# First image of a two-layer attention network: order of normalising and table eviction, and where and when the bias rows are loaded and turned

## The chip, the cores and the metric

The kernel runs on one core of one Trainium2 chip. The metric is the device time of one execution in microseconds, as the median of several runs. The engines are TensorE (PE, matrix products; PEld is its weight loading), VectorE (DVE), ScalarE (ACT), GpSimd (POOL) and SyncE (SP), which here only issues DMAs. Each engine works through its own list of instructions in order, and semaphores hold an instruction until what it needs is there.

## The reference, cut to what matters

There are two layers on x of shape (8, 384, 32, 32). The change lies in the first one: group norm, attention of 8 heads of 48 over 1024 tokens with a relative bias, an output product and a residual.

```python
rel = (coords[:, None, :] - coords[None, :, :]) / denom      # coords of 32 x 32 positions
bias = gelu(rel @ mlp_w1 + mlp_b1) @ mlp_w2 + mlp_b2         # (1024, 1024, 8)
qkv = tokens(_gn(x)) @ qkv_w + qkv_b
attn = softmax(einsum('bhnd,bhmd->bhnm', q * scale, k) + transpose(bias, (2, 0, 1)))
x = x + from_tokens(einsum('bhnm,bhmd->bhnd', attn, v) @ proj_w + proj_b)
```

The bias of a pair of positions depends only on their distance in both directions, so that 63 x 63 = 3969 values for each of the 8 heads hold all of it. The second layer (a second attention and a feed-forward part) is untouched.

## The kernel before, in words

**Table and bias rows.** The 3969 bias values per head come out of a small perceptron at the start: `hidden(r)` computes the hidden units of half r of the distances on TensorE, with a gelu on ScalarE; `table_part(r, hids)` (L272 to L291) multiplies them with the second matrix, evicts the sum on VectorE in reversed order (`part`, L284) and stores it with four DMAs to the table in DRAM (L288). From the table, `grow` is built in SBUF: for each of 128 partitions (4 rows of 32 keys) and each head, 60 rows of 32 bias values. A quarter of a head, 15 rows, is a *part*; there are 8 x 4 = 32 parts. `grow_part(h, c)` (L293 to L308) takes a tile `wide` of the pool of score tiles, fills it with four DMAs of 114.2 KB, each shifted by one element per partition (L300), and then copies it reversed, or *turned*, into its place in `grow`: on ScalarE for even quarters (L306), on VectorE for odd ones (L308). One pool of nine buffers (`etile`) holds hidden units, `wide` tiles and exponentials of scores.

**Group norm.** `group_norm(b, xn)` returns five stages: the statistics of the three channel blocks on VectorE (L323, three stages; the third also sends them through DRAM so that groups stand together, L327 and L331), `scatter`, which combines them on VectorE and POOL and sends scale and shift back (L345, L349), and `apply`, which normalises three blocks (L353), for image 0 on VectorE, for the others on POOL.

**Projection and units.** `project_qk` computes three pairs of heads for queries and keys (L372, six blocks of twelve products; queries are evicted on VectorE, L382, keys on ScalarE, L386) and after each pair rearranges rows by two DMAs (L389); the fourth pair is gathered out of these rows. `project_v` computes the values in four blocks (L400, L405). An image's attention then is 32 *units* (4 pairs x 2 halves of the queries x 4 groups of keys). `scores` makes two PSUM tiles of scores (L426), adds the bias (L437, VectorE) and takes exponentials (L441, ScalarE); `weigh` (L457), two units later, multiplies with the values. The four PSUM tiles of two banks each are shared by all products. After the eighth unit of a pair, its outputs go to `oT[:, pair]` (L465, L468) and `divide` sends the row sums to DRAM and back (L483, L485), inverts them on POOL (L486), stores them (L487) and later spreads and multiplies them (L494, L498).

**What sets the order.** The order on every engine is written out by hand (`manual_schedule`): instructions stand in the order in which the Python code issues them. `later.after(n, work)` issues `work` at the n-th next `later.step()`. In image 0 there are six steps in `project_qk`, four in `project_v` and one after each unit, so that step 11 follows unit 0. The dependences between instructions are found from what they read and write. All DMAs here are issued on SP's queue, in this order too.

Before the change the parts are issued whole (load, then turn) at steps 1 to 22: two at each of the first ten steps, one at each of the other twelve. Image b + 1 is loaded after unit 1 of image b, and its group norm stages come 5, 6, 7, 10 and 13 steps on.

Of the kernel before, what the change touches and what calls it, by code (L numbers as in the profile page):

```python
# [27 lines left out]
P = 128  # L28
QP = P // 2
B, C, IH, IW = 8, 384, 32, 32  # L30
# [10 lines left out]
NF0 = NP0 - 1  # L41
# [3 lines left out]
RW = 2 * IW - 1  # L45
# [51 lines left out]
def _layer0(tc, ins, x1, flag):  # L97
# [6 lines left out]
    with ExitStack() as ctx:  # L104
# [8 lines left out]
        def mm2(name):  # L113
            return ps.tile([P, NH, HALF], F32, tag="p", name=name)

        def etile(name, shape=(P, N)):
            return ep.tile(list(shape), F32, tag="e", name=name)
# [4 lines left out]
        later = _Later()  # L122
# [10 lines left out]
        def backwards(last, *dims):  # L133

            dims = [(1, n) if isinstance(n, int) else n for n in dims]
            return bass.AP(last.tensor, last.offset, [last.ap[0]] + [[-s, n] for s, n in dims])
# [13 lines left out]
        for g in range(P // QT):  # L150
            at = g * QN
            n = min(QN, NREL - at)
# [48 lines left out]
        def place_weights_qk():  # L201
            whole = 2 * NF0 * D0
            for s in range(2):
                nc.vector.tensor_copy(
                    wqk[:, :, s, :, 0:D0],
                    raw[:, :, s, 0:whole].rearrange("p k (h d) -> p k h d", d=D0),
                )
                for j in range(2):
                    at = whole + j * D0
                    nc.vector.tensor_copy(  # L210
                        wqk[:, :, s, j::2, D0:S0],
                        raw[:, :, s, at : at + D0].rearrange("p k (c d) -> p k c d", d=FR),
                    )

        def load_bias_qk():
            with nc.allow_non_contiguous_dma(reason="a bias, once"):
                for j in range(2):
                    for row, n, at, step in (
                        (j * S0, D0, j * D0, 2 * D0),
                        (j * S0 + D0, FR, (2 * NF0 + j) * D0, FR),  # L220
                    ):
                        for s in range(2):
                            nc.sync.dma_start(
                                bqk[row : row + n, s],
                                bass.AP(
                                    qkv_b.tensor, qkv_b.offset + s * C + at, [[1, n], [step, NF0]]
                                ),
                            )

        def load_weights_v_out():  # L230
            nc.sync.dma_start(wv, qkv_w[:, 2 * C : 3 * C].rearrange("(k p) c -> p k c", p=P))
            nc.sync.dma_start(bv, qkv_b[2 * C : 3 * C].partition_broadcast(P))
            pw = ins["L0_conv_proj_w"]
            for j in range(2):
                last = (2 * NF0 + j) * D0
                for row, n, at, step in (
                    (j * S0 + SP, D0, j * D0, 2 * D0),
                    (j * S0, FR, last, FR),
                ):
                    nc.sync.dma_start(  # L240
                        wp[row : row + n],
                        bass.AP(
                            pw.tensor, pw.offset + at * C, [[C, n], [step * C, NF0], [1, C]]
                        ),
                    )
                nc.sync.dma_start(wl[j * S0 + SP : (j + 1) * S0], pw[last : last + D0])
            with nc.allow_non_contiguous_dma(reason="a bias, once"):
                nc.sync.dma_start(bp, ins["L0_conv_proj_b"].rearrange("(k p) -> p k", p=P))

        oT = const.tile([P, NP0, N], F32, tag="oT", name="oT")  # L250
        sums = const.tile([P, B, NP0, 2 * N // P], F32, tag="sums", name="sums")

        WR = GW // 4

        def hidden(r):

            hids = {}
            for k in range(2):
                for a in range(2):
                    ph = mm2(f"ph{r}{k}{a}")  # L260
                    for i in range(2):
                        g = 2 * a + i
                        nc.tensor.matmul(
                            ph[0:HC, i], w1[g * QT : g * QT + 2, ts(k, HC)],
                            rel[g * QT : g * QT + 2, ts(r, HALF)], start=True, stop=True,
                        )
                    hid = etile(f"hid{r}{k}{a}", (HC, 2, HALF))
                    nc.scalar.activation(
                        hid.rearrange("p i q -> p (i q)"), ph[0:HC].rearrange("p i q -> p (i q)"),
                        AF.Gelu, bias=b1[:, k : k + 1],  # L270
                    )
                    hids[k, a] = hid  # L272
            return hids

        def table_part(r, hids):
            pb = mm2(f"pb{r}")
            for k in range(2):
                for g in range(P // QT):
                    nc.tensor.matmul(
                        pb[ts(g, QT), 0], w2[:, k, :], hids[k, g // 2][:, g % 2],  # L280
                        start=(k == 0), stop=(k == 1),
                    )
            part = etile(f"part{r}", (P, HALF))
            nc.vector.tensor_scalar_add(backwards(part[:, HALF - 1 : HALF], HALF), pb[:, 0], b2)  # L284
            for g in range(P // QT):
                at = g * QN + r * HALF
                n = min(HALF, NREL - at)
                nc.sync.dma_start(  # L288
                    table[:, NREL - at - n : NREL - at],
                    part[g * QT : g * QT + H0, HALF - n : HALF],  # L290
                )  # L291

        def grow_part(h, c):  # L293

            run = (WR - 1) * RW + IW
            wide = etile(f"wide{h}_{c}", (P, WR, RW))
            for dy in range(QROWS):
                src = table[h : h + 1, :]
                at = src.offset + NREL - 1 - (WR * (c + 1) + QROWS - 2 - dy) * RW - 2 * (IW - 1)
                nc.sync.dma_start(  # L300
                    wide[ts(dy, IW)].rearrange("p w c -> p (w c)")[:, :run],
                    bass.AP(src.tensor, at, [[1, IW], [1, run]]),
                )
            turned = backwards(wide[:, WR - 1, IW - 1 : IW], (RW, WR), IW)
            if c % 2 == 0:
                nc.scalar.copy(grow[:, h, ts(c, WR), :], turned)  # L306
            else:
                nc.vector.tensor_copy(grow[:, h, ts(c, WR), :], turned)  # L308
# [237 lines left out]
        with tc.manual_schedule():  # L546
            stages = group_norm(0, first)
            for stage in stages[:3]:
                stage()
            place_weights_qk()  # L550
            hids = [hidden(r) for r in range(2)]
            stages[3]()
            load_bias_qk()
            for r in range(2):
                table_part(r, hids[r])
            stages[4](nc.vector)
            load_weights_v_out()
            parts = [(h, c) for h in range(H0) for c in range(4)]

            def grow_parts(n):  # L560
                for _ in range(n):
                    grow_part(*parts.pop(0))

            for i in range(22):
                later.after(i + 1, lambda i=i: grow_parts(2 if i < 10 else 1))
            qk = project_qk(0, first)
            project_v(0, first)
            for b in range(B):
                held = []
                for i, u in enumerate(units):  # L570
                    done = held.pop(0) if len(held) == LAG else None
                    held.append(
                        (u, scores(b, qk, u, lambda: weigh(b, *done) if done else None))
                    )
                    if i == 1 and b + 1 < B:
                        xn = load(b + 1)
                        for at, stage in zip((5, 6, 7, 10, 13), group_norm(b + 1, xn)):
                            later.after(at, stage)
                    if i == 3 and b > 0:
                        project_out(b - 1)  # L580
                    later.step()
                if b + 1 < B:
                    qk = project_qk(b + 1, xn)
                for done in held:
                    finish = weigh(b, *done)
                    if finish is not None:
                        finish()
                if b + 1 < B:
                    project_v(b + 1, xn)
            project_out(B - 1, apart=True)  # L590
# [1062 lines left out]
```

## Time and profile before

| what | before |
|---|---|
| median of 3 runs | 3165.62 us (3164.66 to 3168.25) |
| the profiled execution's own time | 3169.41 us |
| its span from the first to the last instruction | 3166.5 us |
| TensorE busy | 3057.7 us (97%) |
| VectorE, ScalarE, POOL busy | 1744.7, 1400.7, 458.8 us |
| mean granted TensorE clock | 0.988 |
| q1, the queue of SP's DMAs | 147.41 MB |

A row of the profile that describes a group reads: start in us, busy time in us, engine, line, operation, output <- input, count, and in brackets how long the engine was idle before it and what ended this. In the table of stretches, each row is a window, its length, the busy time of each engine with its number of instructions, the granted TensorE clock as a share of full speed, the mean busy share of the 16 DMA engines and GB/s. The stages of image 0 in this execution: projection from 28.12, values from 60.79, scores from 76.37, and the projection of image 1 at 217.68 us.

### The profile page before, as it was taken

The page shows a single profiled execution, that of the slowest core. Times are in us where ns is not written, and L with a number is a line of the kernel's source. Part 1 is how long each engine was busy: PE and PEld are TensorE (multiplying, and loading weights), DVE is VectorE, ACT ScalarE, POOL GpSimd, SP SyncE. Part 2 cuts the span into 40 slices and gives each one's busy share as a digit, 9 for nine tenths or more (in the row PEclk, how much of TensorE's full clock was granted, in tenths as well). Part 3 has the DMA queues.
Part 4 walks back from the last instruction along what each step waited for, and adds up shares of the span by engine and source line. Part 5 has one row for each costly group of instructions (what it writes and reads, how often), then busy time and mean ns, then how long its engine had stood idle before and what let it go on. Part 6 is the DMA issues. An engine that isn't in the chain of part 4 may idle for free.

```text
span 3166.5 us, 46012 instructions
## 1 busy us (share of the span) xinstructions
PE 3057.7 (97%) x19066; PEld 1572.0 (50%) x19066; DVE 1744.7 (55%) x1748; ACT 1400.7 (44%) x1763; POOL 458.8 (14%) x302
## 2 busy tenths in 40 slices
PE   8799999999999999996899999999999999999999
PEld 3254645455555546432445645645645555634343
DVE  2554737373645647273464764754754854844545
ACT  2452616252543526162272462553553643643535
POOL 0110202111111102021200301301201201211110
PEclk9899999999999999998999999999999999999999
DMA  7302020211212020203310110100101101101011
GB/s 178 107 18 79 22 82 16 69 35 25 73 23 81 19 79 22 62 16 105 75 42 22 44 33 22 62 17 21 61 22 27 51 22 29 53 18 62 15 49 42
DMA packets 102768, 150.49 MB, mean 48 GB/s; under 512 B 62260, under 2 KB 65828, under 8 KB 101784
## 3 DMA queue, kind: packets, MB, share of 16 engines
q1 hardware_dynamic: 99688, 147.41, 16.5%
q8 instruction: 153, 2.51, 0.3%
q14 instruction: 63, 0.52, 0.1%
q10 hardware_dynamic: 2864, 0.05, 0.1%
HBM read 111.05 MB, written 27.32 MB: 44 GB/s over the span
## 4 chain that ended last, share of the span: by engine, by line
PE 42%; DVE 4%; DMA 3%; ACT 2%; issue 1%; POOL 1%; SPq 0%; DVEq 0%; ACTq 0%; POOLq 0%
PE s L1168 11%; PE o L1217 10%; PE y2p L1419 5%; PE pq L1023 5%; PE pp L1279 4%; PE y1p L1365 3%; PE pv L1104 3%; POOL hc L1073 1%; PE sum L1240 1%; DVE lun L1319 1%; DVE un L1314 1%; DVE un L1311 1%; DMA rb<-rd 1%; PE tsa L992 1%; PE hs L1052 0%
## 5 line engine op out<-in xcount | busy, mean ns | idle before, releaser
L441 ACT ACTIVATE e<-e 128x1024 f32<-128x1024 f32 x512 | 534.8, 1056 | 461.6 <-DVE e L437 445.6
L437 DVE TENSOR_TENSOR e<-s,grow 128x1024 f32<-128x1024 f32 x512 | 601.1, 1218 | 190.6 <-PE s L426 186.9
L426 PE MATMUL s<-qk 48*64 48x512 f32 x4096 | 613.8, 595 | 23.3 <-DVE e L437 20.3
L457 PE MATMUL o<-e,v 64*64 64x512 f32 x4096 | 608.5, 592 | 0.0
L1179 ACT ACTIVATE e<-s,kc 128x512 f32<-128x512 f32 x768 | 463.5, 691 | 213.3 <-PE s L1168 195.3
L1168 PE MATMUL s<-qk,qk 64*64 64x512 f32 x3072 | 400.6, 601 | 9.9 <-DVE v L1114 9.1
L1217 PE MATMUL o<-e,v 64*64 64x512 f32 x3072 | 391.6, 591 | 0.2 <-ACT e L1179 0.2
L426 PEld LDWEIGHTS s<-qk 48*64 48x64 f32 x4096 | 232.3, 133 | 259.4 <-issue 92.8
L457 PEld LDWEIGHTS o<-e,v 64*64 64x64 f32 x4096 | 249.3, 134 | 192.6 <-issue 96.2
L1194 DVE TENSOR_TENSOR t<-t,e 128x1024 f32<-128x1024 f32 x192 | 231.3, 1222 | 79.2 <-ACT e L1179 79.2
L1023 PE MATMUL pq<-bx,L_attn_qkv_wT 128*128 128x512 f32 x576 | 254.4, 596 | 2.3 <-DVE L_attn_qkv_wT L979 2.1
L372 PE MATMUL pq<-xn,wqk 128*128 128x512 f32 x576 | 251.0, 597 | 1.8 <-DVE xn L353 1.8
L1168 PEld LDWEIGHTS s<-qk,qk 64*64 64x64 f32 x3072 | 146.0, 134 | 211.5 <-issue 128.2
L486 POOL TENSOR_TENSOR inv<-sums,over 128x16 f32<-128x16 f32 x32 | 92.9, 2904 | 1033.1 <-DMA sums<-sd 927.1
L1217 PEld LDWEIGHTS o<-e,v 64*64 64x64 f32 x3072 | 138.8, 133 | 191.4 <-issue 164.6
L372 PEld LDWEIGHTS pq<-xn,wqk 128*128 128x128 f32 x576 | 109.4, 191 | 143.6 <-issue 142.9
L1023 PEld LDWEIGHTS pq<-bx,L_attn_qkv_wT 128*128 128x128 f32 x576 | 107.7, 190 | 145.7 <-issue 140.4
L1191 DVE TENSOR_TENSOR t<-e,e 128x1024 f32<-128x1024 f32 x96 | 114.1, 1224 | 84.1 <-ACT e L1179 84.1
L1352 DVE TENSOR_REDUCE parts<-y 128x1 f32<-128x1024 f32 x75 | 90.0, 1218 | 95.2 <-ACT y L1349 95.0
L1073 POOL TENSOR_TENSOR hc<-hc,rsqrt 128x32 f32<-128x32 f32 x24 | 135.3, 5639 | 2.0
L1039 ACT ACTIVATE qsq<-pq 128x1024 f32<-128x1024 f32 x48 | 49.1, 1024 | 192.5 <-DVE qk L1033 92.1
L1104 PE MATMUL pv<-L_attn_qkv_wT,bx 128*128 128x384 f32 x384 | 130.9, 497 | 1.9 <-DVE meanL_ffn_W1T L1144 1.9
(149 smaller groups left out, 2935.3 us busy)
## 6 DMA issues: line engine op xcount, KB each, us to landing
rb<-rd SPq DMA_DIRECT2D x112, 256.0 KB
wide<-table SPq DMA_DIRECT2D x128, 114.2 KB
xn<-in_x_dram SPq DMA_DIRECT2D x24, 512.0 KB
res<-in_x_dram SPq DMA_DIRECT2D x24, 512.0 KB
x<-res SPq DMA_DIRECT2D x24, 512.0 KB
bx<-x SPq DMA_DIRECT2D x8, 1536.0 KB
rq<-hi SPq DMA_DIRECT2D x48, 256.0 KB
out_dram<-bx SPq DMA_DIRECT2D x24, 512.0 KB
```

Of the source, the lines that this page charges most:

```text
L372: nc.tensor.matmul(pq[:, h], wqk[:, k, s, 2 * pair : 2 * pair + 2, :].rearrange("p h d -> p (h d)"), xn[:, k, ts(h, HALF)], start=(k == 0) ...
L426: nc.tensor.matmul(s[j][ts(c, QP), i], qk[pair][rows, 1, ts(4 * m2 + 2 * i + c, QP)], qk[pair][rows, 0, ts(h, HALF)], start=True, stop=True,)
L437: nc.vector.tensor_add(e.rearrange("p (i q) -> p i q", i=2), s[j], bass.AP(near.tensor, near.offset, [near.ap[0], [-QROWS * IW, 2], [1, HA ...
L441: nc.scalar.activation(e, e, AF.Exp)
L457: nc.tensor.matmul(po[ts(j, S0), r], v[keys, 2 * m2 + i, 2 * pair + j, :], es[j][keys, ts(i, HALF)], start=(m2 == 0 and i == 0), stop=(m2 ...
L1023: nc.tensor.matmul(pq[:, h], wqkv[:, k, s * C + pair * P : s * C + (pair + 1) * P], xt[:, k, ts(h, HALF)], start=(k == 0), stop=(k == KC - 1),
L1073: nc.gpsimd.tensor_tensor(c, c, rsqrt.to_broadcast(list(c.shape)), ALU.pow)
L1104: nc.tensor.matmul(pv[:, i, 0:C], xt[:, k].rearrange("c (p m) -> c m p", m=MT)[:, 2 * m2 + i], wqkv[:, k, 2 * C : 3 * C], start=(k == 0), ...
L1168: nc.tensor.matmul(s[j][ts(c, QP), i], qk[pair, 1][rows, ts(4 * m2 + 2 * i + c, QP)], qk[pair, 0][rows, ts(h, HALF)], start=True, stop=True,)
L1179: nc.scalar.activation(e[:, ts(i, HALF)], s[j][:, i], AF.Exp, scale=kc[:, pair, j, m : m + 1])
L1194: nc.vector.tensor_add(total[j], total[j], e)
L1217: nc.tensor.matmul(po[ts(j, D1), r], v[keys, 2 * m2 + i, at : at + D1], es[j][keys, ts(i, HALF)], start=(m2 == 0 and i == 0), stop=(m2 == ...
```

## The change

`table_part(1)` is issued at step 1, behind the first block of the projection, and image 0 is normalised before `table_part(0)`; the weights for the values and the output are loaded ahead of the stores of the table. `grow_part` is split into `grow_load`, which issues the four DMAs, and `grow_turn`, the reversed copy. Of the 32 parts, 21 are loaded into pool tiles as before, at steps 2 to 10 (3, 3, 2, 3, 2, 2, 2, 2, 2), and each group is turned one step after it was loaded. The other 11 are loaded at steps 9 to 19, one at a step, into `oT[:, 1]`, `oT[:, 2]` and `oT[:, 3]` in turn (the outputs of pairs 1 to 3 are written there later), and a turn follows two steps after its load, at steps 11 to 21. Parts are loaded and turned in one order, first in, first out. For image 0 only, the next image is loaded after unit 8 and not after unit 1, and its group norm moves with it.

```diff
-        def grow_part(h, c):
+        def grow_load(h, c, staged):
 
             run = (WR - 1) * RW + IW
-            wide = etile(f"wide{h}_{c}", (P, WR, RW))
+            wide = oT[:, staged, 0 : WR * RW] if staged else etile(f"wide{h}_{c}", (P, WR * RW))
             for dy in range(QROWS):
                 src = table[h : h + 1, :]
                 at = src.offset + NREL - 1 - (WR * (c + 1) + QROWS - 2 - dy) * RW - 2 * (IW - 1)
                 nc.sync.dma_start(
-                    wide[ts(dy, IW)].rearrange("p w c -> p (w c)")[:, :run],
-                    bass.AP(src.tensor, at, [[1, IW], [1, run]]),
-                )
-            turned = backwards(wide[:, WR - 1, IW - 1 : IW], (RW, WR), IW)
+                    wide[ts(dy, IW), 0:run], bass.AP(src.tensor, at, [[1, IW], [1, run]])
+                )
+            return wide
+
+        def grow_turn(h, c, wide):
+
+            last = (WR - 1) * RW + IW - 1
+            turned = backwards(wide[:, last : last + 1], (RW, WR), IW)
             if c % 2 == 0:
                 nc.scalar.copy(grow[:, h, ts(c, WR), :], turned)
             else:
...
             load_bias_qk()
-            for r in range(2):
-                table_part(r, hids[r])
             stages[4](nc.vector)
             load_weights_v_out()
+            table_part(0, hids[0])
+            later.after(1, lambda: table_part(1, hids[1]))
             parts = [(h, c) for h in range(H0) for c in range(4)]
-
-            def grow_parts(n):
+            waiting = []
+
+            def grow_loads(n, staged=None):
                 for _ in range(n):
-                    grow_part(*parts.pop(0))
-
-            for i in range(22):
-                later.after(i + 1, lambda i=i: grow_parts(2 if i < 10 else 1))
+                    part = parts.pop(0)
+                    waiting.append((*part, grow_load(*part, staged)))
+
+            def grow_turns(n):
+                for _ in range(n):
+                    grow_turn(*waiting.pop(0))
...
+            for i, n in enumerate((3, 3, 2, 3, 2, 2, 2, 2, 2)):
+                later.after(i + 3, lambda n=n: grow_turns(n))
+                later.after(i + 2, lambda n=n: grow_loads(n))
+            for i in range(len(parts) - 21):
+                later.after(i + 11, lambda: grow_turns(1))
+                later.after(i + 9, lambda i=i: grow_loads(1, 1 + i % NF0))
             qk = project_qk(0, first)
             project_v(0, first)
...
-                    if i == 1 and b + 1 < B:
+                    if i == (8 if b == 0 else 1) and b + 1 < B:
                         xn = load(b + 1)
```

## The prediction

> **What bounds the kernel now.** First the page: which engine is full, and where it is not.
>
> ```profile
> PE   8799999999999999996899999999999999999999
> DMA  7302020211212020203310110100101101101011
> ```
>
> TensorE is the bound nearly everywhere; only the first two slices (158 us), which the change touches, and the switch of layers fall off. So I read next the table of five-microsecond stretches over the first 170 us (engine busy times, granted clock, DMA share, GB/s).
>
> ```profile
> 75.00:80.00 5.00, 4.15 (x23) 1.33 (x21) 2.56 (x5) 0.59 (x1) 0.00 (x0) 1.00 1.06 244
> 90.00:95.00 5.00, 2.00 (x20) 0.81 (x16) 2.09 (x3) 0.27 (x1) 0.00 (x0) 0.84 0.79 194
> 95.00:100.00 5.00, 5.00 (x28) 1.36 (x28) 2.29 (x3) 2.53 (x4) 0.00 (x0) 0.50 0.01 2
> 130.00:135.00 5.00, 0.00 (x0) 0.00 (x0) 0.00 (x0) 0.00 (x0) 2.92 (x1) 0.64 0.02 2
> 160.00:165.00 5.00, 5.00 (x52) 3.19 (x48) 2.84 (x3) 3.17 (x3) 0.00 (x0) 1.00 0.00 0
> ```
>
> Up to 85 us the DMA engines are full; at 130 everything stands still with the DMA idle; from 160 TensorE is full at full clock. The order of time of TensorE gives the gaps, that of VectorE and of SP's queue their causes:
>
> ```profile
> 94.75 2.83 PE L426 MATMUL s<-qk 48*64 48x512 f32 x11 [3.00 <-DVE e L437]
> 141.17 2.83 PE L426 MATMUL s<-qk 48*64 48x512 f32 x11 [11.68 <-DVE e L437]
> 217.68 31.17 PE L372 MATMUL pq<-xn,wqk 128*128 128x512 f32 x72
> ```
> ```profile
> 83.38 0.65 DVE L308 COPY grow<-wide 128x480 f32<-128x480 f32 x1 [2.78 <-DMA wide<-table]
> 92.91 0.65 DVE L308 COPY grow<-wide 128x480 f32<-128x480 f32 x1 [4.36 <-DMA wide<-table]
> 139.33 0.65 DVE L308 COPY grow<-wide 128x480 f32<-128x480 f32 x1 [10.96 <-DMA wide<-table]
> ```
> ```profile
> 34.40 9.28 SPq L300 DMA_DIRECT2D wide<-table  x16
> 81.91 2.31 SPq L167 DMA_DIRECT2D xn<-in_x_dram  x3
> 134.63 0.34 SPq L487 DMA_DIRECT2D rd<-inv  x1
> 135.10 4.09 SPq L300 DMA_DIRECT2D wide<-table  x8
> ```
>
> So the add of scores and bias (L437) is late because a turning copy ahead of it on VectorE waits for its load. At 92.91 the load stands behind image 1's input (81.91); at 139.33 it stands in SP's queue behind the divide of pair 0, whose rd store waits for POOL until 134.6. Undisturbed, a unit (two score tiles and their weighing) takes 3.435 us (s blocks at 207.00, 210.44, 213.87).
>
> **The change, step by step.** Times are on this profiled execution (time 3169.41, span 3166.5, so 2.9 around it; the median of the runs, 3165.62, is 3.8 lower). I subtract the saved microseconds from the median.
>
> *Front.* The scales gsc were issued at 17.93; in image 1 such a load was used 2.1 us after its issue (145.86 to 148.00), so 20.1; three normalising operations take 2.25 (L353), done at 22.3. The first half's table products end at 23.4 (pb, 32 in 6.46, 3.2 for a half; part at 23.60). Projection can start at 23.4, not 28.12. Step 1 costs 5.2 (31.17/6), then the second half's 3.2: 31.8. Five more steps (26.0) and project_v (15.64, its waits included) end at 73.4 instead of 76.4. Of these 3.0, 1.8 are the gap before 28.12 and the rest its low clock (0.68 in 28.1:33.4). This gain is **hidden**: the first scores wait for the turns anyway.
>
> *SP and the table.* Bias issues end at 22.15. Weights are now ahead of the table: 28.60 to 33.18 is 4.6, giving 26.7; the first half's four stores 2.1, to 28.8. The second half's part is ready at 31.8 + 0.9 = 32.7; four stores (1.4 to 2.1) and a landing of 1.6 (there, 118.82+0.38 to 120.78) put the first wide load at 36.0, against 34.40: **1.6 late**.
>
> *The early loads.* The loads are four DMAs of 114.2 KB (0.468 MB a part). In before the turns run from 40.41 to 83.38, 20 parts: 2.1 a part plus 1.2 at each of three qk copies in the queue (40.4 + 19·2.1 + 3.6 = 83.9). This pace is of the DMA engines (share near 1, 240 GB/s), so loading a step ahead doesn't raise it. Now part n is ready at 42.0 + 2.1n + 3.6. Unit 0's adds stand behind turn 17 on VectorE: 81.3, hence adds at 82.0 to 84.3 (before 83.95). Step 11 then turns three parts (19, 20, 21): part 21 at 89.7, copied by 90.4. Unit 1's adds, before at 86.3, come **4 us later**. Behind them waits the first weighing: four PSUM tiles hold units 0 and 1; unit 2's scores take unit 0's two, and the accumulator needs unit 1's first, free at 90.4 + 1.2 = 91.6. By the queue's order three blocks of 1.72 follow before unit 4's scores: 96.8 at full clock.
>
> *Clock.* The Trainium skill (TensorE: Matmul & The Clock Gate, Part 1) says that the clock halves after an idle window of about 3.4 us and returns after as much sustained work. Here the row differs: after only 3.00 us idle the clock was 0.50 from 95 to 100, and two blocks, 3.44 at full clock, took from 94.75 to 100.75: 2.6 lost. By the rule the gap left before 91.6 (some 2.6 us) is free and the saving of the whole change is 23.5; by the row it costs 2.6. I take the row: unit 4 starts at 99.4, against 100.74 before: **1.3 gained**.
>
> *DMA rule.* The skill (DMA: Bandwidth & Descriptors, Specifications) gives 358 GB/s as a core's HBM limit: 1.3 us a part (an estimate), part 21 at 73, no wait in unit 1, unit 4 at about 87 and a saving of 33. The measured 2.1 decides; I use 33 only as the outer bound.
>
> *From unit 4 on.* Before: 100.74 to 217.68 is 116.94. Needed: 28 units · 3.435 = 96.2, plus 1.1 of gaps (0.72 and 0.34) which the statistics of image 1 on VectorE leave (they move from units 6–8 to 12–14). So **19.6 gained**, if the parts come in time. Per unit the loads need 2.1 of 3.44. A staged load waits for the turn three parts earlier and is turned three units later: 10.3 us, against 2.1 issue + 4.2 landing (first load after 34.4 + 2.0, turn at 40.41): 4 us of margin. The last load is issued before unit 9's divide, so the stand at 130 goes. In place of it stands image 1's input ahead of that last load: 1.5 MB, 5 to 6.6 us at 240 to 320 GB/s; it starts near 113, the last part lands at 121 to 123.5, its turn is due near 123.7: from 0 to 1 us, I take 0. The places in oT free buffers for e: worth nothing, since in the waits only SP's own loads waited for a weighing to free one.
>
> *Image 1's norm.* It moves by seven units: scatter at 17, apply at 20. POOL does 3.54 us of apply and shares units 17 to 22 with pair 1's divide (2.9) and product (2.4); projection needs it after unit 31, 11 units or 38 us later. Covered; without that cover it would cost up to 24 us (7 · 3.44). The bn_aggr on VectorE stands at unit 17 in front of unit 18's adds; its gather was issued three units earlier. The turns' copies, loads and all other instructions are the same in number.
>
> Sum: 1.3 + 19.6 = 20.9; **3144.7**.
>
> **Rivals.** (a) *More is gained*: the low clock doesn't come, or loads begin earlier or flow faster (320 GB/s were seen in 85:90): 23.5 to 28, 3138 to 3142. For: spread of the clock; against: twenty equal turns. (b) *Late staged turns*: the 4 us of margin goes, for example by landing slower while small DMAs share SP, and each of nine turns costs 1 us, or the last waits 5 us behind the input: saving 8 to 15, 3151 to 3158. (c) *Nothing measurable*: SP still gets stuck, or TensorE loses the time again before image 1's projection: 3160 to 3170. Against: 38 us of slack there. (d) *Slower*: the staged loads go one at a time, because the places lie in one tile oT and a load waits for any turn out of it. Then each part takes 2.1 + 4.2 + 0.65 = 7 us against 3.44, ten times: 35 lost, minus 20.9: 3180. It decides at a round of 5.5 us. Against: at 210.94 a POOL product on oT's pair 2 and the copy into pair 3, written earlier in the program, start together, and at 86–88 an add read grow while ScalarE wrote another part of it.
>
> **Chances and range.** Forecast 0.62, (a) 0.13, (b) 0.14, (c) 0.06, (d) 0.05. The forecast's own range is 3141 to 3148: start of loads ±1.5, clock 2.6, last part 1, unit ±1. The range to 3138 takes all of (a) but its end and to 3154 the nearer half of (b). A change under 0.2% (6.3 us) can't be told from none. Faster: 0.62 + 0.13 + 0.14 = 0.89; same 0.06; slower 0.05.
>
> **What would show it.** Projection starts near 23.4; first wide load near 36; unit 1's adds near 90; all 32 turns over by 125 and no stand at 130; no wide load behind rd; image 1's projection near 197; the input of image 1 issued near 113. Wrong if turns in units 4 to 10 still end VectorE's idle time, if unit 1's adds come well after 92, or if image 1's projection waits for xn.

## The result, and the profile after

The changed kernel takes 3144.40 us (median; 3140.00 to 3145.32) against 3165.35 for the kernel before. The ratio is 0.9929, with a 95% interval from 0.9912 to 0.9947: 0.7% faster, 20.95 us by the medians, where 20.9 was forecast; by the ratio it is 22.5. Of the two profiled executions the spans differ by 23.5 us (3166.5 and 3143.0); the profiled execution of before took 3169.41 us, 4.1 more than the median.

The stretches of five microseconds that were shown of before, now of the changed kernel (window, length, busy time of PE, PEld, DVE, ACT and POOL, granted clock, DMA share, GB/s):

```profile
75.00:80.00 5.00, 2.95 (x17) 0.78 (x16) 2.98 (x5) 0.79 (x2) 0.00 (x0) 0.98 1.05 238
85.00:90.00 5.00, 2.26 (x12) 0.88 (x16) 4.19 (x5) 2.29 (x3) 0.00 (x0) 0.50 0.81 229
95.00:100.00 5.00, 5.00 (x52) 2.02 (x48) 3.98 (x5) 3.63 (x4) 0.00 (x0) 1.00 0.15 46
130.00:135.00 5.00, 5.00 (x46) 2.04 (x45) 4.96 (x6) 3.39 (x4) 2.38 (x1) 1.00 0.01 2
160.00:165.00 5.00, 5.00 (x52) 3.05 (x48) 3.75 (x4) 3.15 (x5) 3.92 (x3) 1.00 0.03 8
```

From 95 us on TensorE is full at full clock, where before it had gaps up to 152 us; the stand at 130 is gone. Two gaps and a stretch at half clock are left between 75 and 95. The order of time of TensorE, VectorE and SP's queue in the changed kernel shows what they wait for:

```profile
79.41 4.81 PE L430 MATMUL s<-qk 48*64 48x512 f32 x16 [1.78 <-DVE e L441]
87.74 3.69 PE L461 MATMUL o<-e,v 64*64 64x512 f32 x16 [3.52 <-DVE e L441]
95.76 1.90 PE L430 MATMUL s<-qk 48*64 48x512 f32 x16
192.71 31.17 PE L376 MATMUL pq<-xn,wqk 128*128 128x512 f32 x72
```
```profile
85.81 0.65 DVE L312 COPY grow<-wide 128x480 f32<-128x480 f32 x1 [2.79 <-DMA wide<-table]
86.38 4.61 DVE L441 TENSOR_TENSOR e<-s,grow 128x1024 f32<-128x1024 f32 x4
120.61 0.64 DVE L312 COPY grow<-oT 128x480 f32<-128x480 f32 x1
```
```profile
33.80 5.40 SPq L300 DMA_DIRECT2D wide<-table  x12
109.53 1.32 SPq L167 DMA_DIRECT2D xn<-in_x_dram  x3
112.04 1.91 SPq L300 DMA_DIRECT2D oT<-table  x4
124.15 0.34 SPq L491 DMA_DIRECT2D rd<-inv  x1
```

The turn at 85.81 is part 21, the third of step 11. It still holds the adds of unit 1, and the first weighing (87.74) waits for these. But the last load (112.04) stands ahead of the divide's rd store, and the last turn on VectorE (120.61) waits for nothing. Image 1's projection starts at 192.71 instead of 217.68. I use this start below: it measures the stage that was changed and is free of what happens in the 2950 us after it.

### The profile page after: what moved, and what is told of

It reads as the page before. It is cut to its first block, busy times and chain, and to the rows that moved or that the text cites. A ratio compares the mean times of both kernels' runs of the same rounds, so it can differ in the third digit from the quotient of the medians.

```text
span 3143.0 us, 46032 instructions
## 1 busy us (share of the span) xinstructions
PE 3053.0 (97%) x19066; PEld 1571.3 (50%) x19066; DVE 1745.3 (56%) x1748; ACT 1401.2 (45%) x1763; POOL 459.2 (15%) x302
## 4 chain that ended last, share of the span: by engine, by line
PE 43%; DVE 4%; DMA 2%; ACT 2%; issue 2%; POOL 1%; SPq 0%; DVEq 0%; ACTq 0%; POOLq 0%
PE s L1184 11%; PE o L1233 10%; PE y2p L1435 5%; PE pq L1039 5%; PE pp L1295 4%; PE y1p L1381 3%; PE pv L1120 3%; POOL hc L1089 1%; PE sum L1256 1%; PE tsa L1008 1%; DVE lun L1335 1%; DVE un L1330 1%; DVE un L1327 1%; DMA rb<-rd 1%; ACT qsq L1055 1%
## 5 line engine op out<-in xcount | busy, mean ns | idle before, releaser
L430 PE MATMUL s<-qk 48*64 48x512 f32 x4096 | 599.1, 593 | 2.0 <-DVE e L441 1.8
L461 PE MATMUL o<-e,v 64*64 64x512 f32 x4096 | 593.9, 591 | 3.5 <-DVE e L441 3.5
L1233 PE MATMUL o<-e,v 64*64 64x512 f32 x3072 | 391.9, 591 | 0.2 <-ACT e L1195 0.2
L1207 DVE TENSOR_TENSOR t<-e,e 128x1024 f32<-128x1024 f32 x96 | 114.2, 1224 | 84.3 <-ACT e L1195 84.0
## 6 DMA issues: line engine op xcount, KB each, us to landing
wide<-table SPq DMA_DIRECT2D x84, 114.2 KB
```

The lines of the kernel that those rows point to most:

```text
L430: nc.tensor.matmul(s[j][ts(c, QP), i], qk[pair][rows, 1, ts(4 * m2 + 2 * i + c, QP)], qk[pair][rows, 0, ts(h, HALF)], start=True, stop=True,)
L461: nc.tensor.matmul(po[ts(j, S0), r], v[keys, 2 * m2 + i, 2 * pair + j, :], es[j][keys, ts(i, HALF)], start=(m2 == 0 and i == 0), stop=(m2 ...
L1233: nc.tensor.matmul(po[ts(j, D1), r], v[keys, 2 * m2 + i, at : at + D1], es[j][keys, ts(i, HALF)], start=(m2 == 0 and i == 0), stop=(m2 == ...
```

## The experiments

The theory T: TensorE's gaps came from turns queued on VectorE or ScalarE ahead of the adds and exponentials, while their loads stood behind other work on SP's queue; loads that run ahead of their turns remove this, and the earlier projection is hidden. The rivals give the gain to another part of the change: to the front (F), to the later load of image 1 (M) or to the outputs' places (O). Two questions are about the forecast's own terms: whether the divide caused the stand (N says no), and what sets the pace of 2.1 us a part (the DMA engines, as forecast, or SP's issue, I).

In these rounds the kernel before took 3169.5 to 3170.8 us, 4 to 5 us more than in the first comparison, while the expectations were written against 3165.4. So I read them by ratio: the last column is the ratio times 3165.35. The start of image 1's projection is that of one profiled execution each; the two of the changed kernel differ by 0.5 us.

| run | image 1's projection, us | median, us | ratio to before (95%) | scaled, us |
|---|---|---|---|---|
| before | 217.7 | – | 1 | 3165.4 |
| changed, first comparison | 192.7 | 3144.40 | 0.9929 (0.9912 to 0.9947) | 3142.9 |
| changed, again (e12) | 193.2 | 3143.94 | 0.9919 (0.9905 to 0.9932) | 3139.7 |
| e1 front undone | 192.3 | 3146.78 | 0.9932 (0.9915 to 0.9948) | 3143.8 |
| e2 image 1 early | 193.1 | 3146.21 | 0.9932 (0.9916 to 0.9949) | 3143.8 |
| e3 pool tiles | 191.8 | 3144.99 | 0.9924 (0.9907 to 0.9940) | 3141.3 |
| e4 front alone | 217.1 | 3168.13 | 0.9993 (0.9985 to 1.0002) | 3163.1 |
| e5 image 1 late alone | 201.7 | 3161.04 | 0.9971 (0.9959 to 0.9983) | 3156.2 |
| e6 last two behind the divide | 204.7 | 3158.29 | 0.9959 (0.9944 to 0.9974) | 3152.4 |
| e7 a third of the bytes | 188.8 | 3141.98 | 0.9916 (0.9898 to 0.9933) | 3138.8 |
| e8 turns spread | 187.3 | 3139.37 | 0.9908 (0.9890 to 0.9926) | 3136.2 |
| e9 two queues | 197.0 | 3153.23 | 0.9946 (0.9933 to 0.9960) | 3148.3 |
| e10 turns spread, all loads before the divide | 184.7 | 3137.90 | 0.9898 (0.9883 to 0.9913) | 3133.1 |
| e11 loads ahead alone | 194.0 | 3146.41 | 0.9924 (0.9910 to 0.9937) | 3141.3 |

**One part undone.** e1 puts the front back, e2 the load of image 1, e3 the pool tiles.

```diff
 e1, against the changed kernel
+            for r in range(2):
+                table_part(r, hids[r])
             stages[4](nc.vector)
             load_weights_v_out()
-            table_part(0, hids[0])
-            later.after(1, lambda: table_part(1, hids[1]))
 e2, against the changed kernel
-                    if i == (8 if b == 0 else 1) and b + 1 < B:
+                    if i == 1 and b + 1 < B:
 e3, against the changed kernel
-                later.after(i + 9, lambda i=i: grow_loads(1, 1 + i % NF0))
+                later.after(i + 9, lambda i=i: grow_loads(1))
```

> The changed kernel with the front as before: both halves of the table evicted and stored first, then image 0 normalised, then the weights loaded. Theory T (the gain comes from loads that no longer stand behind other work when their turn is due; the earlier projection is hidden): first scores at 76 instead of 72.6 us, first wide load near 34.4 instead of 33.8 but beside the weights, so unit 1's adds at 86 to 89; time 3144 to 3147. Rival F (the earlier projection, 5 us, is part of the gain): 3149 or more.

> The changed kernel with image 1 loaded after unit 1 again and its group norm at the old places. Theory T: the input (about 6 us of transfer) stands in the queue between staged loads near 85 us; their two steps of lead (6.9 us) take up most of it; time 3144 to 3148. Rival M (the later load of image 1 is a large part of the gain): 3150 or more.

> The changed kernel with the last 11 parts loaded into pool tiles at the same steps, not into the outputs' places. Theory T: the lead decides, not the place; nine buffers hold three units at three tiles each, so a load waits for the weighing of an earlier unit and loses some of its lead; time 3144 to 3148. Rival O (the outputs' places are what gives the lead): 3152 to 3165.

Image 1's projection starts at 192.3, 193.1 and 191.8 us, all within 0.9 us of the changed kernel's 192.7, and the ratios agree. F, M in its form "without it the gain is lost", and O fall. (The scaled times lie 0.2, 0.2 and 2.7 us below the ranges given for T, on the side away from the rivals.) In e1 the first scores do start later, at 75.06 against 72.63, but the order of time of TensorE gives nearly the same moment for the first weighing (87.74 in the changed kernel):

```profile
80.91 4.82 PE L430 MATMUL s<-qk 48*64 48x512 f32 x16 [2.18 <-DVE e L441]
88.58 3.56 PE L461 MATMUL o<-e,v 64*64 64x512 f32 x16 [2.86 <-DVE e L441]
```

The earlier projection is hidden, as forecast: it waits longer at the turns.

**One part alone.** e4 is the kernel before with the new front, e5 with the later load of image 1 (their diffs are those of e1 and e2 the other way round), e11 with the split into loads and turns and their new steps: the changed kernel with the edits of e1, e2 and e3 made together.

> The kernel before with the new front alone (image 0 normalised ahead of the table's evictions, second half of the table behind the first projection block, weights ahead of the stores). Theory T: turns up to unit 1 come some 2 us sooner because the first loads no longer meet the weights; the stand behind the divide stays near 11 us; time 3162 to 3165.5. Rival F: 3160 or less.

> The kernel before with image 1 loaded after unit 8 instead of unit 1, and nothing else. Theory T: the stall of 4.4 us at unit 2 goes, but the input then stands ahead of the last four parts, which are turned in the step of their load, so 5 to 7 us come back there and the stand behind the divide stays; time 3162 to 3169. Rival M: 3160 or less.

> The kernel before with the split into loads and turns alone: the new steps for both, all parts in pool tiles, image 1 loaded after unit 1 and the front as before. If the read-ahead alone carries the gain, as the runs with one part undone suggest: image 1's projection at 192 to 195 us, time within 3 us of the changed kernel's. If the later load of image 1 is needed for a share of it (it alone gave 16 of 25 us to the projection of image 1): 205 to 210 us, time 10 us or more above the changed kernel's.

The front alone moves image 1's projection by 0.6 us and the time not measurably. The loads ahead, alone (e11), move it by 23.7 of the 25.0 us: they carry the gain.

```profile
194.00 31.17 PE L376 MATMUL pq<-xn,wqk 128*128 128x512 f32 x72
```

e5 missed its expectation: I gave the later load of image 1 nothing on balance, and it alone moves the projection by 16.0 us and the time by 0.29%, as M has it. Of the 16.0 us, 9.5 are there by unit 4's scores (91.27 against 100.74); the other 6.5 were not taken apart. The order of time of e5 (TensorE, then VectorE):

```profile
83.09 2.64 PE L426 MATMUL s<-qk 48*64 48x512 f32 x13 [1.74 <-DVE e L437]
127.14 2.83 PE L426 MATMUL s<-qk 48*64 48x512 f32 x11 [10.37 <-DVE e L437]
```
```profile
86.35 0.65 DVE L308 COPY grow<-wide 128x480 f32<-128x480 f32 x1
125.30 0.65 DVE L308 COPY grow<-wide 128x480 f32<-128x480 f32 x1 [10.80 <-DMA wide<-table]
```

Without the image's input in SP's queue, the old order has its loads early by itself: the turn at 86.35 waits for nothing, where the one at 92.91 had waited 4.36 us, and the gap of 3.00 us with the half clock behind it is gone. The stand behind the divide stays, nearly whole. What I expected to come back, 5 to 7 us of input ahead of the last four parts, doesn't show: the input was issued at 103.98 while the queue was ahead of its steps. The two parts overlap, so what each gives alone (16.0 and 23.7) is more than the 25.0 of both; beside the loads ahead, the later image is worth less than can be measured (e2).

**The divide.** e6 takes the lead away from the last two parts only, so that their loads come behind the divide again.

```diff
-                later.after(i + 11, lambda: grow_turns(1))
-                later.after(i + 9, lambda i=i: grow_loads(1, 1 + i % NF0))
+                if i < 9:
+                    later.after(i + 11, lambda: grow_turns(1))
+                later.after(i + (9 if i < 9 else 11), lambda i=i: grow_loads(1, 1 + i % NF0))
+                if i >= 9:
+                    later.after(i + 11, lambda: grow_turns(1))
```

> The changed kernel with the last two of the 32 parts loaded and turned in one step, at steps 20 and 21, so that their loads are issued behind the divide of pair 0. Theory T: the loads wait for POOL's inversion until about 124.5 us, the turn lands near 130 and the adds of units 10 and 11 stand for it: a stand of 6 to 9 us and a low clock after it; time 3152 to 3156. Rival N (the divide was not what held TensorE): under 3147.

The order of time of SP's queue, VectorE and TensorE in e6:

```profile
124.00 0.34 SPq L491 DMA_DIRECT2D rd<-inv  x1
124.39 3.95 SPq L300 DMA_DIRECT2D oT<-table  x8
```
```profile
130.78 0.65 DVE L312 COPY grow<-oT 128x480 f32<-128x480 f32 x1 [10.19 <-DMA oT<-table]
```
```profile
132.62 2.83 PE L430 MATMUL s<-qk 48*64 48x512 f32 x11 [8.44 <-DVE e L441]
```

The stand is back with the same chain: inversion on POOL (121.06 to 123.98), rd, load, turn, add, 8.44 us of idle TensorE and eleven products in 2.83 us after it. Image 1's projection comes 12.0 us later and the scaled time, 3152.4, is inside the expected 3152 to 3156. N falls.

**The pace of the loads.** e7 keeps the number and the rows of the DMAs and moves a third of the bytes.

```diff
-            run = (WR - 1) * RW + IW
+            run = (WR // 3 - 1) * RW + IW
...
-            last = (WR - 1) * RW + IW - 1
-            turned = backwards(wide[:, last : last + 1], (RW, WR), IW)
+            last = (WR // 3 - 1) * RW + IW - 1
+            turned = backwards(wide[:, last : last + 1], (0, 3), (RW, WR // 3), IW)
+            place = grow[:, h, ts(c, WR), :].rearrange("p (a w) x -> p a w x", a=3)
```

> The changed kernel with the same 128 loads of a third of the bytes: each part loads five rows and its turn repeats them three times, so two thirds of the bias rows hold values of other rows. Theory T (units 0 to 2 wait for the DMA engines' rate, 2.1 us a part): the parts come at 1.3 to 1.7 us, no turn delays unit 1, unit 4's scores start near 86 to 88 instead of 95.8; time 3134 to 3138. Rival I (the pace is SP's issue, four DMAs of 0.5 us a part, whatever their size): 3143 to 3146.

In stretches of ten microseconds, first the changed kernel, then e7:

```profile
60.00:70.00 10.00, 10.00 (x33) 5.89 (x32) 3.69 (x7) 1.19 (x2) 0.00 (x0) 1.00 1.05 220
```
```profile
60.00:70.00 10.00, 10.00 (x33) 5.89 (x32) 4.28 (x8) 1.19 (x2) 0.00 (x0) 1.00 0.43 92
```

The DMA share falls from 1.05 to 0.43. The issues hardly change; SP's queue and VectorE in the changed kernel, then in e7:

```profile
63.47 12.26 SPq L300 DMA_DIRECT2D wide<-table  x24
```
```profile
62.42 11.64 SPq L300 DMA_DIRECT2D wide<-table  x24
82.44 0.65 DVE L313 COPY grow<-wide 128x480 f32<-128x480 f32 x1 [3.05 <-DMA wide<-table]
```

24 issues, one behind the other, take 11.64 us instead of 12.26, so 0.485 us each instead of 0.51. The four of a part take 1.94 us instead of 2.04, and part 21 is turned at 82.44 instead of 85.81. Theory T expected 1.3 to 1.7 us a part and unit 1 free: missed. The scaled time, 3138.8, lies in neither range (T up to 3138, I from 3143). The pace hardly follows the bytes; in e7 it is SP's issue, as the rival I has it, and with all bytes the issues come only 5% slower. The DMA share of 1.05 at 220 GB/s did not by itself show a limit in bytes: where image 1's input flows (110 to 115 us in the changed kernel) the share is 0.98 at 335 GB/s. The 3.9 us by which image 1's projection is earlier are mostly part 21's 3.4, of a slightly faster pace and an earlier landing.

e9 was to lift the issue instead, by a second queue:

```diff
-                nc.sync.dma_start(
+                queue = nc.scalar if dy % 2 and not staged else nc.sync
+                queue.dma_start(
```

> The changed kernel with two of the four DMAs of each of the first 21 pool-tile parts issued from ScalarE's queue, the others from SP's; bytes, order and turns are the same. Theory I (the pace of 2.1 us a part is SP's issue, 4 times 0.5 us): the pace falls to 1.1 to 1.5 us, no turn of step 11 delays unit 1, image 1's projection starts at 184 to 188 instead of 192.7 us; time 5 to 9 us under the changed kernel's on the same chip. Rival T (the DMA engines' rate, their share was at 1.04): the pace stays at 2.0 to 2.1 us and the time within 2 us of the changed kernel's.

Both expectations missed: image 1's projection is 3.8 us later than in e12, and the median 9.3 us longer (the spans of the two profiled executions differ by 4.4; the rest was not traced to anything). The order of time of ScalarE and its queue shows that the experiment made a wait of its own:

```profile
62.36 1.96 ACTq L301 DMA_DIRECT2D wide<-table  x4
68.92 0.59 ACT L311 COPY grow<-wide 128x480 f32<-128x480 f32 x1 [6.04 <-DMA wide<-table]
69.00 1.73 ACTq L301 DMA_DIRECT2D wide<-table  x4
```

ScalarE issues the next loads only after its turn, and the turn waits for the loads before. The run decides nothing on I. What stays open is how much faster the parts would come with the issue out of the way and all bytes moved: with a DMA share of 1.05 the engines may be near the same pace.

**Turns that wait for nothing.** If the loads come at 2.1 us and units pass at 3.44, no turn has to be issued before its part can be there. e8 keeps the loads up to step 11 and spreads the turns; e10 corrects the last steps, so that all loads are ahead of the divide.

```diff
 e8, against the changed kernel
-            for i, n in enumerate((3, 3, 2, 3, 2, 2, 2, 2, 2)):
+            for i, n in enumerate((3, 3, 2, 3, 1, 1, 2, 1, 1, 2, 2, 1) + 10 * (1,)):
                 later.after(i + 3, lambda n=n: grow_turns(n))
+            for i, n in enumerate((3, 3, 2, 3, 2, 2, 2, 2, 2)):
                 later.after(i + 2, lambda n=n: grow_loads(n))
-            for i in range(len(parts) - 21):
-                later.after(i + 11, lambda: grow_turns(1))
-                later.after(i + 9, lambda i=i: grow_loads(1, 1 + i % NF0))
+            for i, at in enumerate((9, 10, 11, 13, 15, 16, 17, 18, 19, 20, 21)):
+                later.after(at, lambda i=i: grow_loads(1, 1 + i % NF0))
 e10, against e8
-            for i, n in enumerate((3, 3, 2, 3, 1, 1, 2, 1, 1, 2, 2, 1) + 10 * (1,)):
+            for i, n in enumerate((3, 3, 2, 3, 1, 1, 2, 1, 1, 2, 2, 1, 2, 1, 1, 2, 1, 1, 1, 1)):
...
-            for i, at in enumerate((9, 10, 11, 13, 15, 16, 17, 18, 19, 20, 21)):
+            for i, at in enumerate((9, 10, 11, 13, 15, 15, 16, 17, 18, 18, 19)):
```

> The changed kernel with the same loads up to step 11 but turned later, one or two at a step, so that no turn is issued before its part can have landed (16 turned by step 10 instead of 19, 17 by step 11 instead of 22, the last at step 24); the last staged loads move by two steps with them and so come behind the divide, three steps ahead of their turn. Theory T: units 0 to 3 run on, unit 4's scores start near 85 to 88, and three steps of lead cover the divide; time 3134 to 3138. Rival W (the wait only moves to later turns): 3142 to 3148.

> The changed kernel with the turns spread as in the run before of that kind, but caught up by two at a step at steps 15 and 18, so that all loads are issued ahead of pair 0's divide again. Expected: the waits of 2.1 and 0.4 us near 124 to 127 us go, image 1's projection starts at 184 to 185.5 instead of 187.3 us; time 8 to 10 us under the changed kernel's on the same chip. Rival W (two turns at a step bring the wait back): 5 to 7 us under.

> The changed kernel as it is, on the same chip and in the same rounds as the three others, for the comparison with them: a ratio of 0.992 to 0.994 to the kernel before.

In e8 the first units run through (unit 4's scores start at 85.09), but two loads stand behind the divide and leave this gap on TensorE, and a low clock a little later; the twelve products of the second line take 1.87 us at full clock:

```profile
127.04 1.53 PE L430 MATMUL s<-qk 48*64 48x512 f32 x11 [2.12 <-DVE e L441]
128.40 3.56 PE L461 MATMUL o<-e,v 64*64 64x512 f32 x12
```

In e10 the only gap of TensorE between the first scores and 132 us is 0.27 us, and the adds of units 0 and 1 follow each other. TensorE, then VectorE:

```profile
118.63 1.51 PE L430 MATMUL s<-qk 48*64 48x512 f32 x11 [0.27 <-DVE e L441]
184.72 31.17 PE L376 MATMUL pq<-xn,wqk 128*128 128x512 f32 x72
```
```profile
77.26 4.62 DVE L441 TENSOR_TENSOR e<-s,grow 128x1024 f32<-128x1024 f32 x4 [0.36 <-issue]
```

Image 1's projection starts at 184.7 us, as expected. The time is 3137.90 us, 6.0 us under e12 on the same chip where 8 to 10 were expected. That number is the one of the rival W (5 to 7), but the wait that W names is not in the trace: the projection gave 8.5, and the spans of the two profiled executions differ by 8.3 (3144.8 and 3136.5), that of e12 being the longest of its five. No run of e10 (up to 3139.05) reaches the fastest of e12 (3142.92), so e10 is faster than both kernels.

## Why the prediction was right

The total was right to 0.1 us by the medians, and its main term, the 19.6 us from unit 4 on, for the reason given. The gain before unit 4 was mis-sized by 3.7 us, and the cause given for the pace of the loads was wrong. Point by point:

- *Front hidden: right.* Projection started at 22.85 (forecast 23.4), the first scores at 72.63 (73.4). Undone (e1) it leaves image 1's projection 0.4 us earlier, alone (e4) it brings it forward by 0.6: nothing either way.
- *First wide load at 36.0: 2.2 us too late.* The landing of 1.6 us was counted from the last of the four stores of the second half. The first load was issued at 33.80, 1.6 after the issue of the first of these stores (32.22). By the code, part 0 reads only columns that lie in this store and in the first half's; the later stores had not to land first.
- *Pace of 2.1 us a part: right in size, wrong in cause.* "This pace is of the DMA engines" failed: with a third of the bytes it was 1.94 against 2.04 (e7). The forecast's outer bound of 1.3 us a part, worked out from bytes, was not reached even with a third of them.
- *From unit 1 to unit 4: 1.3 us forecast, 5.0 measured* (95.76 against 100.74). This is the mis-sized term. Part 21 was copied by 86.46, not 90.4: 2.2 us from the start of the loads and the rest from the first landing, about 4 us after the first issue (37.93) and not the 6 taken from before. There the weights were still in transfer (from 30 to 35 us the DMA share was 0.98, here 0.16), which fits but is not shown by a run. The mechanism, three turns at step 11 and the accumulator waiting for unit 1's first score tile, was as forecast, and e8 shows that with the turns spread, one at that step, the gap goes. The low clock came too, but earlier than forecast: it was 0.50 from 80 us on, behind the gap of 1.78 us, and stayed so through the next. The blocks from 87.74 to 95.76 took 8.0 us where three need 5.2: 2.9 lost, 2.6 forecast.
- *From unit 4 on: 19.6 forecast, 20.0 measured* (192.71 − 95.76 = 96.95, against 116.94). The two sources named, the stand behind the divide and late turns, are shown by e6 and e11; the staged turns had their margin, and the input of image 1 (109.53, forecast near 113) cost nothing.
- *One tile for three places: no round trip.* Rival (d) did not come: e3, without these places, starts image 1's projection 0.9 us earlier, so they neither serialise nor help measurably.
- *Sum.* By the trace the stage gave 25.0 us, 4.1 more than forecast. After image 1's projection the two profiled executions take 2948.8 and 2950.3 us; these 1.5 us were not traced to anything. The exact agreement of the medians is in part luck: by the trace the sum was 4.1 us short, by the ratio 1.6.

## What to carry to other kernels

Where an engine takes its work in order, a copy that waits for a load holds all that stands behind it: issue the load steps ahead, the copy when the data can be there, and keep loads ahead of any store in the same queue that waits for a slow chain. Before paying for "wider" or "earlier", find what sets the pace of a stream: a full DMA share does not say that the bytes do it. And when several edits remove the same wait, try each alone and each undone, since the shares do not add up.

## What the runs showed of the hardware that I had not expected

- DMAs of 32 rows from DRAM to SBUF left SP's queue every 0.485 us when they moved 35.5 KB and every 0.51 us when they moved 114.2 KB, while the DMA share went from 0.43 to 1.05 (e7).
- Gaps of TensorE of about 2 us were followed by half the clock, and not always at once. In the changed kernel 1.78 us of idle TensorE before 79.41 were followed by a granted clock of 0.50 from 80 to 90. In e8 2.12 us before 127.04 were followed by eleven products in 1.53 us, as in e10 at a clock of 1.00 (1.51), and only then by twelve products in 3.56 us; the granted clock was 1.00 up to 128 and 0.50 from 129 to 131. The gap of 0.27 us in e10 left it at 1.00. What sets the delay was not tested.
